# Graph attention weights as a larger of two products of exponentials, and the adjacency check on ScalarE

## The chip, the cores and the metric

The kernel runs on one core of one Trainium2 chip. The metric is the device time of a launch in microseconds, as the median of three runs. Lower is better. The core's engines are PE (TensorE: matrix products), DVE (VectorE), ACT (ScalarE), POOL (GpSimd) and SP (SyncE, which here only starts transfers); each works through its own list of instructions in order, and they meet through semaphores.

## The reference, cut to what matters

The input is x with 64 graphs of 256 nodes and 256 features, all fp32, and an adjacency of 0 and 1 (int32, about one in sixteen set). Two layers follow each other. Layer 0 runs two graph attentions, a norm, a feed-forward block and a norm. Layer 1 is an attention of eight heads in which the adjacency chooses among value matrices, again with a feed-forward block. The change concerns the graph attention and what the kernel must know of the adjacency:

```python
def _gat(h, adj, W, a, out_features):
    Wh = jnp.matmul(h, W)
    Wh1 = jnp.matmul(Wh, a[:out_features])
    Wh2 = jnp.matmul(Wh, a[out_features:])
    e = Wh1 + jnp.swapaxes(Wh2, 1, 2)
    e = jax.nn.leaky_relu(e, negative_slope=ALPHA)      # ALPHA = 0.2
    scores = jnp.where(adj > 0, e, NEG)
    att = jax.nn.softmax(scores, axis=1)
    return jnp.matmul(att, Wh)
```

So a weight is exp(max(t, 0.2 t)) with t = r + c, r a number of the row and c one of the column, times the adjacency, divided by its sum over the first node axis.

## The kernel before

The kernel has a quick path, `narrow_path`, which holds for adjacencies of 0 and 1 and for numbers that need no maximum subtracted, and a `general_path` for everything else. The quick path sums up on the way what tells whether it held: `other` collects the sums of a(a - 1) over the adjacency, `low`, `lowg` and `high` those of reciprocals and means. At the end the results of these sums decide whether the general path runs; with this input it doesn't.

The 64 graphs are taken in 32 pairs u. A pair is two graphs, so 512 nodes in T = 4 blocks of 128 partitions; NB = 2 blocks to a graph. Work is spread over three pairs at a time. The function `turn(y, x, z)` runs one turn: it does layer 1 of pair y, the feed-forward block of layer 0 of pair x = y + 1, and both graph attentions of pair z = y + 2. There are 32 turns; 30 have a pair z. An opening ahead of them brings the first two pairs so far.

Inside a turn the order of PE, SP, DVE and ACT is the order in which the code is written (`manual_schedule`), so each engine's list can be read off `turn`. In the opening only PE and SP follow the code; a scheduler orders DVE and ACT there.

A graph attention's softmax is the class `Softmax`. `score_rows` lays the row numbers r out in a bank of PSUM by four transposes (`rows`), a column number c per node stands in the projected features. `scores(b)` writes r + c for graph b (L741: ACT, Identity with the column as bias, one of 128x256 for each block) and takes the larger of it and 0.2 of it (L743: DVE, 128x512). `exp(b)` is L746 (ACT, 128x512). `masks(b)` multiplies by the transposed adjacency and sums along the way (L750: DVE, 128x256 for each block). `shares` takes the reciprocals (L754: DVE), and `scaled` multiplies the features by them (L766: ACT, four of 128x256).

In a turn with a pair z, this happens twice, each time in the middle of a feed-forward output. `HiddenOut` computes such an output with seven products instead of eight: `sums(n)` forms a sum of quarters on DVE (L946, 128x1024), `product(n)` is sixteen matmuls on PE (L960), `add(n)` adds a product to the output on DVE (L968); `out(n)` is a product and its add. Products share banks: 6 follows 1 in its bank, 7 follows 6, 4 follows 7, and 3 follows 5; each needs the add before it. Product 7 reads sum 3, product 3 reads sum 4.

First place (layer-1 attention of pair z, inside pair x's output): scores and exponentials stand at L1291 to 1294, then sum 4, products 2 and 5, the norm of y (`applied_norm`, L1300), masks, shares and scaling (L1302 to 1305), product 6, the features' transposes of y (`normed_features`: four transposes on DVE, L668, then copies on POOL and transfers from SP's and ACT's queues, L685 and L687), product 3, sum 3, and the products of the attention (`first_sums`, L775) with product 7 between their halves.

Second place (layer-2 attention, inside pair y's output): L1371 to 1396. Scores of both graphs lie among the adds of products 1 and 5, masks after product 2 and product 6, then shares and scaling. At the end come the check of the adjacency (`checked`, L706: one operation of 128x1024 on DVE), the loads of the next adjacency (eight transfers on SP, L449, into the tile that the check read and overwrote), and the products of the attention (`second_sums`, L786), whose result is normed for the next turn.

The other names that the prediction uses: L883 and L880 bring products of the first feed-forward half out of PSUM, L889 and L914 are its activation (gelu in layer 1, with a load of its table; exp needs another), L821 is the small operation `nm` of a norm, L986 are the query and key products (`qp`, `kp`) with which a turn begins, L988 their copies, L1021 the exponentials of the head attention.

Of the kernel before, what the change touches and what calls it, by code (L numbers as in the profile page):

```python
# [9 lines left out]
F32 = mybir.dt.float32  # L10
I32 = mybir.dt.int32
AF = mybir.ActivationFunctionType
ALU = mybir.AluOpType
# [3 lines left out]
P = 128  # L17
NEG = -9000000000000000.0
ALPHA = 0.2
# [366 lines left out]
def narrow_path(  # L386
# [13 lines left out]
    nc = tc.nc  # L400
    B, N, F = x.shape
# [5 lines left out]
    NB = N // P  # L407
    G = 2
    T = G * NB
    TN = G * N  # L410
    NG = B // G
# [7 lines left out]
    work = ctx.enter_context(tc.tile_pool(name="work", bufs=2))  # L419
# [50 lines left out]
    mhalf = const.tile([P, T], F32, name="mhalf")  # L470
# [10 lines left out]
    other = const.tile([P, NG], F32, name="other")  # L481
# [63 lines left out]
    g = {u: {} for u in range(NG)}  # L545
# [94 lines left out]
    def behind(*names):  # L640

        stack = ExitStack()
        for n in names:
            stack.enter_context(tc.issue_after(mark[n].ins))
        return stack
# [57 lines left out]

    def checked(u, aq):
        a = aq.rearrange("p t n -> p (t n)")
        nc.vector.scalar_tensor_tensor(a, a, 1.0, a, op0=ALU.subtract, op1=ALU.mult,  # L706
                                       accum_out=other[:, u:u + 1])

    def projected(u, hT, blocks, xp):
        if xp is None:  # L710
# [17 lines left out]
    class Softmax:  # L728

        def __init__(s, u, l, wh, rows, c):  # L730
            s.u, s.wh, s.rows, s.c = u, wh, rows, c
            s.s = (work.tile([P, T, N], F32, tag="s", name=f"s{u}_{l}", bufs=1) if u > 1 else
                   work.tile([P, 2 * T, N], F32, tag="e", name=f"s{u}_{l}")[:, :T])
            s.z = work.tile([P, T], F32, tag="z", name=f"z{u}_{l}")

        def block(s, b):
            return s.s[:, b * NB:(b + 1) * NB, :].rearrange("p t n -> p (t n)")

        def scores(s, b):
            for t in range(b * NB, (b + 1) * NB):  # L740
                nc.scalar.activation(s.s[:, t, :], s.rows[:, b * N:(b + 1) * N], AF.Identity,  # L741
                                     bias=s.wh[:, t, s.c:s.c + 1])
            nc.vector.scalar_tensor_tensor(s.block(b), s.block(b), ALPHA, s.block(b), op0=ALU.mult, op1=ALU.max)  # L743

        def exp(s, b):
            nc.scalar.activation(s.block(b), s.block(b), AF.Exp)  # L746

        def masks(s, b):
            for t in range(b * NB, (b + 1) * NB):
                nc.vector.scalar_tensor_tensor(s.s[:, t, :], s.s[:, t, :], 1.0, g[s.u]["aT"][:, t, :],  # L750
                                               op0=ALU.mult, op1=ALU.mult, accum_out=s.z[:, t:t + 1])
# [3 lines left out]
            nc.gpsimd.tensor_add(lowg, lowg, s.z)  # L755

        def all(s):
            for b in range(G):
                s.scores(b)
                s.exp(b)  # L760
                s.masks(b)
            s.shares()

# [27 lines left out]
    def normed(u, l, y, blocks=range(T)):  # L791

        applied_norm(y, *norm(u, l, y, blocks))

    def moments(u, l, y, blocks, mv=None):
        n = f"{u}_{l}_{blocks[0]}"
        st = work.tile([P, T, 6], F32, tag="st", name=f"st{n}", bufs=1)
        if mv is None:
            mv = work.tile([P, T, 2], F32, tag="mv", name=f"mv{n}")
        for t in blocks:  # L800
            nc.vector.bn_stats(st[:, t, :], y[:, t, :])  # L801
            nc.vector.bn_aggr(mv[:, t, :], st[:, t, :])  # L802
        return mv

    def norm(u, l, y, blocks=range(T), mv=None):

        n, t0 = f"{u}_{l}_{blocks[0]}", blocks[0]
        bt = slice(t0, t0 + len(blocks))
        mv = moments(u, l, y, blocks if mv is None else blocks[len(blocks) // 2:], mv)
        rs = work.tile([P, T], F32, tag="rs", name=f"rs{n}")  # L810
        nm = work.tile([P, T], F32, tag="nm", name=f"nm{n}")
        nc.gpsimd.tensor_scalar(rs[:, bt], mv[:, bt, 1], EPS, 0.0, op0=ALU.add, op1=ALU.add)  # L812
        nc.gpsimd.tensor_tensor(rs[:, bt], rs[:, bt], mhalf[:, bt], ALU.pow)  # L813
        if l == 3:
            nc.gpsimd.tensor_add(high[:, bt], high[:, bt], mv[:, bt, 0])
        return blocks, mv, rs, nm
# [279 lines left out]
    def first_sums(z, blocks=range(T)):  # L1096
        d = g[z]
        d["hp"] = gat_first(z, d["m"].s, d["xp"], None if blocks[0] == 0 else d["hp"], blocks)

    def second_sums(z, graphs=range(G)):  # L1100
        d = g[z]
        mv = None
        for b in graphs:
            add_blocks(z, "ygp", d["y"], b,
                       lambda t, k: d["m"].s[:, t // NB * NB + k, t % NB * P:(t % NB + 1) * P],
                       lambda b, k: d["hp"][:, b * NB + k, :F], NB)
            if b == 0 and len(graphs) == G:
                mv = moments(z, 0, d["y"], range(NB))
        return mv
# [45 lines left out]
    def turn(y_, x_, z):  # L1155
        Y, X, Z = (g.get(u) for u in (y_, x_, z))
# [41 lines left out]
        with order:  # L1198
# [70 lines left out]
            else:  # L1269
                n = norm(y_, 2, y, range(NB))  # L1270
# [13 lines left out]
            if Z:  # L1284
                n = norm(y_, 2, y, mv=mv)
            else:
                applied_norm(y, *n)
                n = norm(y_, 2, y, range(NB, T))
            if Z:
                out(1)  # L1290
                Z["m"].scores(0)  # L1291
                Z["m"].scores(1)
                Z["m"].exp(0)
                Z["m"].exp(1)
                out.sums(4)
                out(2, 5)
            elif X:
                out(5)
                out.sums(3)
# [30 lines left out]
            if X:  # L1330
                n = moments(x_, 1, X["y"], range(NB))
# [6 lines left out]
            if X:  # L1338
                out.add(4)
                n = norm(x_, 1, X["y"], mv=n)  # L1340
# [31 lines left out]
            out = HiddenOut(y_, 1, y, h1, w2s, out_sums(y_, 1))  # L1372
            out.product(1)
            out.sums(1, 2)
            Z["m"].scores(0)
            out.add(1)
            out.product(5)
            Z["m"].scores(1)
            Z["m"].exp(0)
            Z["m"].exp(1)  # L1380
            out.add(5)
            out.sums(4, 3)
            out(2)
# [5 lines left out]
            out(3)  # L1389
            affine(X["y"], rg2, rb2)  # L1390
            out(7)
            checked(z, Z["aq"])
            if z + 1 < NG:
                load_adjacency(z + 1)
            Z["n"] = norm(z, 0, Z["y"], mv=second_sums(z))
            out(4)
            waiting.append((y_, y))
# [3 lines left out]
    with tc.manual_schedule(engines={mybir.EngineType.PE, mybir.EngineType.SP}):  # L1401
        for stage in (early_first, project, first_softmax):
            stage(0)
        early_first(1)
        next(fold)
        for stage in (project, first_softmax):
            stage(1)
        first_sums(0)
        next(fold)
        second_softmax(0)  # L1410
        first_sums(1)
        next(fold)
        second_softmax(1)
        for b in range(G):
            second_sums(0, (b,))
            normed(0, 0, g[0]["y"], range(b * NB, (b + 1) * NB))
        next(fold)
        g[0]["hT"] = to_features(g[0]["y"], "h1T0")
        with behind("summed"):
            for u in range(2):  # L1420
                checked(u, g[u]["aq"])
        affine(g[0]["y"], rg1, rb1)
        load_x(2)
        load_rows(2)
        load_adjacency(2)
        first_hidden(0)("2a 1a 2b 1b 5a 5b 3a 3b 6a ra 6b rb 7a sa 7b sb 4a 4b")
        first = HiddenOut(0, 0, g[0]["y"], g[0]["h1"], wf2s, out_sums(0, 0))
        first.sums(1, 2, 4, 3)
        first(1, 2, 5, 6, 3)
        normed(0, 1, g[0]["y"], range(NB))  # L1430
        first(7, 4)
        normed(0, 1, g[0]["y"], range(NB, T))
        g[1]["n"] = norm(1, 0, g[1]["y"], mv=second_sums(1))
        g[0]["hT"] = to_features(g[0]["y"], "h2T0")
        affine(g[0]["y"], rg2, rb2)
        next(fold)
        for u in range(NG):
            turn(u, u + 1, u + 2)


    c = work.tile([P, 4], F32, tag="mv", name="checks")
    for n, v in enumerate((low, lowg, high, other)):
        nc.vector.tensor_reduce(c[:, n:n + 1], v, AX.X, ALU.add)
    s = work.tile([P, 1], F32, tag="ve", name="checked")
    nc.vector.tensor_reduce(s, c[:, 0:3], AX.X, ALU.add)
    good = work.tile([P, 2], F32, tag="z", name="good")
    nc.vector.tensor_scalar(good[:, 0:1], s, 1e30, None, op0=ALU.is_le)
    nc.vector.tensor_scalar(good[:, 1:2], c[:, 3:4], 0.0, None, op0=ALU.is_le)
    nc.vector.tensor_tensor(good[:, 0:1], good[:, 0:1], good[:, 1:2], ALU.mult)
    ps = bank("goodp")  # L1450
    nc.tensor.matmul(ps[:1, :1], good[:, 0:1], ones[:, 0:1], start=True, stop=True)
# [41 lines left out]
```

## Time and profile before

| what | value |
|---|---|
| median of 3 runs | 3076.99 us (3075.04 to 3077.49) |
| profiled execution, span | 3072.8 us, the only time that the page gives for it |
| median above the span | 4.2 us |
| PE busy | 3031.3 us, 99% |
| DVE busy | 2595.7 us, 84% |
| ACT busy | 1602.2 us, 52% |
| POOL busy | 648.0 us, 21% |
| a steady turn | 93.44 us (1331.4 to 1424.9) |
| L750, masks | 256 of 128x256, 97.1 us, mean 424 ns |
| L743, larger of two | 128 of 128x512, 92.4 us, mean 742 ns |
| L741, sums of row and column | 256 of 128x256, 100.2 us |
| L746, exponentials | 128 of 128x512, 76.5 us, mean 627 ns |
| L706, check of the adjacency | 32 of 128x1024, 38.9 us |

The profile is of one execution on the chip. Busy shares are averages over the span; the slices on its page cut the span into 40 parts and give the busy share of each in tenths. A line of the time line has start, duration, engine, line of the code, operation, output and input, shapes, count, and in brackets how long the engine stood idle before it and what ended that. Where operations follow each other without a wait, the next starts before the end of the one before, so in a row they cost less than their durations. PEld is the loading of the stationary operand, which runs ahead of the matmuls.

### The profile page before, as it was taken

What the parts mean: (1) busy time and instruction counts of PE and PEld (TensorE: products, weight loads), DVE (VectorE), ACT (ScalarE), POOL (GpSimd) and SP (SyncE); (2) the same over time, 40 slices, a digit from 0 to 9 for tenths busy, and PEclk for the clock granted to TensorE, in tenths of its full rate; (3) what the DMA queues carried; (4) which work ended last, traced back from release to release, by engine and by line L of the source; (5) the groups of instructions that cost most, each with busy time, mean ns of one, the idle gap of its engine ahead of it and who ended that gap; (6) DMA issues with size and microseconds to landing.
All of it is one profiled execution on the core that took longest, in us unless ns stands there. A gap on an engine that the chain in (4) does not pass through costs nothing.

```text
span 3072.8 us, 56424 instructions
## 1 busy us (share of the span) xinstructions
PE 3031.3 (99%) x21432; PEld 2330.1 (76%) x21432; DVE 2595.7 (84%) x4890; ACT 1602.2 (52%) x3212; POOL 648.0 (21%) x896
## 2 busy tenths in 40 slices
PE   7999999999999999999999999999999999999998
PEld 6677877778777778777787777787777787777866
DVE  4788888888888888888888888888888888888876
ACT  4455545555545555555555455555455554554553
POOL 3122121222211221212221112222112212122211
PEclk8999999999999999999999999999999999999999
DMA  5011111211111211112211112111112111121000
GB/s 149 13 37 35 34 39 25 44 41 35 35 35 32 44 37 32 39 26 43 44 33 35 40 25 44 37 36 35 30 38 44 35 34 39 25 44 37 18 13 16
DMA packets 427988, 113.37 MB, mean 37 GB/s; under 512 B 364568, under 2 KB 427072, under 8 KB 427712
## 3 DMA queue, kind: packets, MB, share of 16 engines
q1 hardware_dynamic: 417664, 102.46, 15.8%
q10 hardware_dynamic: 8992, 6.19, 0.8%
q8 instruction: 172, 2.82, 0.4%
q0 software_dynamic: 1056, 1.05, 0.1%
q14 instruction: 104, 0.85, 0.1%
HBM read 57.04 MB, written 16.78 MB: 24 GB/s over the span
## 4 chain that ended last, share of the span: by engine, by line
PE 90%; DVE 7%; DMA 1%; POOL 1%; ACT 1%; issue 0%; SPq 0%; ACTq 0%; POOLq 0%; DVEq 0%
PE yf L960 22%; PE h1a L871 15%; PE h1b L871 11%; PE po L1041 8%; PE vp L999 7%; PE sp L1015 4%; PE xpp L715 4%; PE yop L786 4%; PE qp L986 3%; PE kp L986 3%; PE ygp L786 3%; PE zo L1044 2%; PE hpp L775 2%; DVE s L750 2%; DVE yt L668 1%; DVE eaq L946 1%
## 5 line engine op out<-in xcount | busy, mean ns | idle before, releaser
L880 ACT COPY h<-h1b 128x512 f32<-128x512 f32 x384 | 224.6, 585 | 390.0 <-PE h1b L871 390.0
L828 ACT ACTIVATE y<-y,nm,rs 128x256 f32<-128x256 f32 x450 | 239.0, 591 | 238.4 <-DVE nm L821 234.1
L883 DVE TENSOR_TENSOR h<-h1a,h 128x512 f32<-128x512 f32 x384 | 263.6, 687 | 117.5 <-PE h1a L871 111.6
L1026 DVE TENSOR_TENSOR ea<-e,aT 128x1024 f32<-128x1024 f32 x256 | 309.5, 1239 | 54.3 <-ACT e L1021 54.3
L1021 ACT ACTIVATE e<-sp 128x512 f32<-128x512 f32 x512 | 264.3, 602 | 52.0 <-PE sp L1015 48.7
L1054 POOL TENSOR_TENSOR low<-low,rq 128x16 f32<-128x16 f32 x64 | 13.9, 218 | 1087.3 <-DVE rq L1053 1087.3
L685 POOL COPY hT<-yt 32x256 f32<-32x256 f32 x244 | 207.2, 849 | 59.0 <-DVE yt L668 51.4
L968 DVE TENSOR_TENSOR y<-yf,y 128x256 f32<-128x256 f32 x448 | 183.1, 409 | 39.7 <-PE yf L960 39.6
L999 PE MATMUL vp<-wv,hT 128*128 128x512 f32 x480 | 214.0, 599 | 0.0
L801 DVE BATCH_NORM_STATS2 st<-y 128x6 f32<-128x256 f32 x512 | 207.7, 408 | 5.5
L812 POOL TENSOR_SCALAR rs<-mv 128x4 f32<-128x4 f32 (+1 forms) x134 | 34.2, 255 | 720.7 <-DVE mv L802 454.6
L999 PEld LDWEIGHTS vp<-wv,hT 128*128 128x128 f32 x480 | 88.7, 190 | 110.4 <-issue 103.2
L840 DVE TENSOR_TENSOR y<-y,rb 128x1024 f32<-128x1024 f32 (+1 forms) x130 | 166.9, 1284 | 3.2
L988 ACT ACTIVATE q<-qp,cols 128x512 f32<-128x512 f32 x64 | 44.0, 687 | 238.3 <-PE qp L986 238.3
L914 ACT ACTIVATE h<-h,cols 128x512 f32<-128x512 f32 x256 | 167.0, 714 | 1.5 <-DVE h L883 1.1
L837 DVE TENSOR_TENSOR y<-y,rg 128x1024 f32<-128x1024 f32 (+1 forms) x130 | 161.8, 1245 | 2.2 <-ACT y L828 1.1
L1031 DVE TENSOR_TENSOR es<-e 128x1024 f32<-128x1024 f32 x128 | 155.5, 1215 | 0.0
L677 POOL COPY hT<-yt 32x256 f32<-32x256 f32 x120 | 115.6, 964 | 169.2 <-DVE yt L668 159.7
L1015 PEld LDWEIGHTS sp<-q,k 32*128 32x128 f32 x2048 | 92.5, 184 | 74.2 <-issue 44.8
L1015 PE MATMUL sp<-q,k 32*128 32x256 f32 x2048 | 146.6, 400 | 2.0 <-ACT k L988 2.0
L1041 PE MATMUL po<-e,v 128*32 128x256 f32 x2048 | 136.3, 384 | 0.0
L813 POOL TENSOR_TENSOR rs<-rs,mhalf 128x4 f32<-128x4 f32 (+1 forms) x134 | 134.5, 1004 | 8.2
(249 smaller groups left out, 7191.4 us busy)
## 6 DMA issues: line engine op xcount, KB each, us to landing
hT<-yt SPq DMA_DIRECT2D x912, 32.0 KB, 2.0
y<-in_x_dram SPq DMA_DIRECT2D x32, 512.0 KB, 4.7
xq<-in_x_dram SPq DMA_DIRECT2D x240, 64.0 KB, 2.2
aq<-in_adj_dram SPq DMA_DIRECT2D x240, 64.0 KB, 2.4
out_dram<-y SPq DMA_DIRECT2D x30, 512.0 KB, 2.9
hT<-yt ACTq DMA_DIRECT2D x180, 32.0 KB, 1.9
wf<-in_L_gnn_w_ff_dram SPq DMA_DIRECT2D x2, 1024.0 KB, 8.1
w<-in_L_gnn_W_dram SPq DMA_DIRECT2D x2, 1024.0 KB
```

Of the source, the lines that this page charges most:

```text
L786: nc.tensor.matmul(ps[:, i * F:(i + 1) * F], lhs(t, k), rhs(b, k), start=(k == 0), stop=(k == n - 1))
L801: nc.vector.bn_stats(st[:, t, :], y[:, t, :])
L828: mark["normed"] = nc.scalar.activation(y[:, t, :], y[:, t, :], AF.Identity, bias=nm[:, t:t + 1], scale=rs[:, t:t + 1])
L871: nc.tensor.matmul(ps[:, i * N:(i + 1) * N], w_[:, f * P:(f + 1) * P], m, start=first and i == 0, stop=True, skip_group_check=True)
L880: mark["copied"] = nc.scalar.copy(out(h, o, b), pair(ps))
L883: mark["added"] = nc.vector.tensor_tensor(out(h, o, b), pair(one[h]), out(h, o, b), ALU.add)
L960: nc.tensor.matmul(s.ps[n][:, i * F2:(i + 1) * F2], a[:, k, i * P:(i + 1) * P], w_[:, k, :], start=n in (1, 2, 5) and i == 0 and k == 0, s ...
L999: nc.tensor.matmul(ps, hT[k][:, t * P:(t + 1) * P], wvf[:, k, :], start=(k == 0), stop=(k == KB - 1))
L1015: nc.tensor.matmul(ps[a][:, j * N:(j + 1) * N], k_[hp, m, j0:j0 + P], q[hp, m, b * N:(b + 1) * N], start=True, stop=True)
L1021: mark[f"exp{b * KB + m}"] = nc.scalar.activation(e[:, a, :], ps[a], AF.Exp, scale=isd)
L1026: nc.vector.tensor_tensor(ea[:, a:a + 2, :], e[:, a:a + 2, :], ab[:, None, :].to_broadcast([P, 2, NB * N]), ALU.mult)
L1041: nc.tensor.matmul(po[hp, m * N:(m + 1) * N], vs[:, hp], w[:, a, j * N:(j + 1) * N], start=(n == 0), stop=(n == len(terms) - 1))
```

## The change

The weight is written with exponentials apart. With E = exp(r) and E' = exp(0.2 r) of the rows and f = exp((0.2 - 1) c) of the columns,

exp(max(t, 0.2 t)) = max(exp(r) exp(c), exp(0.2 r) exp(0.2 c)) = exp(c) max(E, E' f),

and exp(c), the same for all that is summed over, drops out in the softmax. So ACT takes one exponential of 4 columns (f) and two of 128x512 (E and E', both graphs at once), and DVE takes max(E' f, E) for each block of 128x256 in one operation. The sums on ACT, the exponentials of full blocks and the maxima of 128x512 go. The four products stand in `masks`, ahead of the masks of the same graph. The new tile `es` shares the two buffers of the head attention's node sums.

The check becomes a Square on ACT: (a - 0.5) squared is 0.25 for 0 and 1 and more for any other integer, so the sum is compared with a quarter of the number of elements. In a turn it moves ahead, behind the exponentials of the second place, and with it the loads of the next adjacency on SP; in the opening it no longer waits to be placed behind a sum.

```diff
     def checked(u, aq):
         a = aq.rearrange("p t n -> p (t n)")
-        nc.vector.scalar_tensor_tensor(a, a, 1.0, a, op0=ALU.subtract, op1=ALU.mult,
-                                       accum_out=other[:, u:u + 1])
+        nc.scalar.activation(a, a, AF.Square, bias=mhalf[:, 0:1], accum_out=other[:, u:u + 1])
...
+            s.e = work.tile([P, 2, TN], F32, tag="es", name=f"er{u}_{l}")
+            s.f = work.tile([P, T], F32, tag="ef", name=f"ef{u}_{l}")
+
+        def exps(s):
+            nc.scalar.activation(s.f, s.wh[:, :, s.c], AF.Exp, scale=ALPHA - 1.0)
+            nc.scalar.activation(s.e[:, 0], s.rows, AF.Exp)
+            nc.scalar.activation(s.e[:, 1], s.rows, AF.Exp, scale=ALPHA)
...
-        def scores(s, b):
+        def masks(s, b):
+            bn = slice(b * N, (b + 1) * N)
             for t in range(b * NB, (b + 1) * NB):
-                nc.scalar.activation(s.s[:, t, :], s.rows[:, b * N:(b + 1) * N], AF.Identity,
-                                     bias=s.wh[:, t, s.c:s.c + 1])
-            nc.vector.scalar_tensor_tensor(s.block(b), s.block(b), ALPHA, s.block(b), op0=ALU.mult, op1=ALU.max)
-
-        def exp(s, b):
-            nc.scalar.activation(s.block(b), s.block(b), AF.Exp)
-
-        def masks(s, b):
+                nc.vector.scalar_tensor_tensor(s.s[:, t, :], s.e[:, 1, bn], s.f[:, t:t + 1], s.e[:, 0, bn],
+                                               op0=ALU.mult, op1=ALU.max)
             for t in range(b * NB, (b + 1) * NB):
                 nc.vector.scalar_tensor_tensor(s.s[:, t, :], s.s[:, t, :], 1.0, g[s.u]["aT"][:, t, :],
                                                op0=ALU.mult, op1=ALU.mult, accum_out=s.z[:, t:t + 1])
...
                 out(1)
-                Z["m"].scores(0)
-                Z["m"].scores(1)
-                Z["m"].exp(0)
-                Z["m"].exp(1)
+                Z["m"].exps()
                 out.sums(4)
                 out(2, 5)
...
             out.sums(1, 2)
-            Z["m"].scores(0)
+            Z["m"].exps()
+            checked(z, Z["aq"])
+            if z + 1 < NG:
+                load_adjacency(z + 1)
             out.add(1)
             out.product(5)
-            Z["m"].scores(1)
-            Z["m"].exp(0)
-            Z["m"].exp(1)
             out.add(5)
...
             out(7)
-            checked(z, Z["aq"])
-            if z + 1 < NG:
-                load_adjacency(z + 1)
             Z["n"] = norm(z, 0, Z["y"], mv=second_sums(z))
...
-        with behind("summed"):
-            for u in range(2):
-                checked(u, g[u]["aq"])
+        for u in range(2):
+            checked(u, g[u]["aq"])
...
-    nc.vector.tensor_scalar(good[:, 1:2], c[:, 3:4], 0.0, None, op0=ALU.is_le)
+    nc.vector.tensor_scalar(good[:, 1:2], c[:, 3:4], 0.25 * NG * T * N, None, op0=ALU.is_le)
```

More of the change, by code (lines that the diff above doesn't have):

```diff
@@ L734, in __init__ @@
             s.z = work.tile([P, T], F32, tag="z", name=f"z{u}_{l}")
-        def block(s, b):
-            return s.s[:, b * NB:(b + 1) * NB, :].rearrange("p t n -> p (t n)")
-        def scores(s, b):
-            for t in range(b * NB, (b + 1) * NB):
-                nc.scalar.activation(s.s[:, t, :], s.rows[:, b * N:(b + 1) * N], AF.Identity,
-                                     bias=s.wh[:, t, s.c:s.c + 1])
-            nc.vector.scalar_tensor_tensor(s.block(b), s.block(b), ALPHA, s.block(b), op0=ALU.mult, op1=ALU.max)
-        def exp(s, b):
-            nc.scalar.activation(s.block(b), s.block(b), AF.Exp)
-        def masks(s, b):
+            s.e = work.tile([P, 2, TN], F32, tag="es", name=f"er{u}_{l}")
[6 more added lines that the diff above has]
+            bn = slice(b * N, (b + 1) * N)
+            for t in range(b * NB, (b + 1) * NB):
+                nc.vector.scalar_tensor_tensor(s.s[:, t, :], s.e[:, 1, bn], s.f[:, t:t + 1], s.e[:, 0, bn],
+                                               op0=ALU.mult, op1=ALU.max)
             for t in range(b * NB, (b + 1) * NB):
@@ L757, in all @@
         def all(s):
+            s.exps()
             for b in range(G):
-                s.scores(b)
-                s.exp(b)
                 s.masks(b)
```

## The prediction

> **What bounds the kernel now.** I read the page first (busy shares and slices), then the waits by engine, then the time line of one steady turn, 1331 to 1425 us, engine by engine.
>
> ```profile
> span 3072.8 us, 56424 instructions
> PE 3031.3 (99%) x21432; PEld 2330.1 (76%) x21432; DVE 2595.7 (84%) x4890; ACT 1602.2 (52%) x3212; POOL 648.0 (21%) x896
> PE   7999999999999999999999999999999999999998
> PEclk8999999999999999999999999999999999999999
> ```
>
> PE is the bound from slice 2 on, at full clock. It has 41.5 us of idle time in all and most of that lies in the opening. A turn takes 93.44 us, so a stall of PE in a turn is not won back later: PE has no slack to win it from. The question is therefore only where PE waits, and for whom, in the two places where a turn runs a graph softmax. The waits give one that repeats in every turn of that kind:
>
> ```profile
> PEld yf L960 <- DVE eaq L946: 15.0, 30, 0.5
> ```
>
> Thirty times, once per turn with a third pair Z. The windows show that it reaches PE itself (columns after the width: PE, PEld, DVE, ACT, POOL busy, then clock, DMA share, GB/s):
>
> ```profile
> 1380.30:1382.29 1.99, 1.90 (x10) 1.33 (x8) 1.99 (x5) 0.83 (x3) 1.48 (x2) 1.00 0.13 30
> 1400.32:1411.51 11.19, 11.19 (x101) 11.19 (x100) 10.62 (x22) 7.30 (x16) 4.07 (x5) 1.00 0.25 38
> ```
>
> DVE is busy for all of the first stretch and PE for 1.90 of 1.99 us; in the second PE never waits. The time line of the first place, the layer-1 softmax:
>
> ```profile
> 1376.92 0.42 DVE L968 TENSOR_TENSOR y<-yf,y 128x256 f32<-128x256 f32 x1 [0.48 <-PE yf L960]
> 1377.33 0.42 DVE L750 SCALAR_TENSOR_TENSOR s<-s,aT 128x256 f32<-128x256 f32 x1
> 1378.83 0.18 DVE L754 RECIPROCAL z<-z 128x4 f32<-128x4 f32 x1
> 1379.43 1.70 ACT L766 ACTIVATE xp<-xp,z 128x258 f32<-128x258 f32 x4
> 1380.30 1.91 PE L775 MATMUL hpp<-xp,s 128*128 128x258 f32 x8
> 1380.88 1.36 DVE L946 TENSOR_TENSOR eaq<-h 128x1024 f32<-128x1024 f32 x1
> 1382.29 1.86 PEld L960 LDWEIGHTS yf<-wf,eaq 128*128 128x128 f32 x16 [0.50 <-DVE eaq L946]
> ```
>
> From the add at 1376.92 on DVE runs without a gap until the quarter sum ends at 1382.24, and product 7 starts at 1382.29. The twin group of eight hpp matmuls goes 1384.18 to 1385.92, 1.74 us; here it is 1.99 to the next start, so PE loses 0.25 us. Anything put on DVE between 1377 and 1382 moves product 7 one for one.
>
> The second place, the layer-2 softmax:
>
> ```profile
> 1404.36 1.95 PE L960 MATMUL yf<-w,h 128*128 128x128 f32 x16
> 1410.10 0.18 DVE L754 RECIPROCAL z<-z 128x4 f32<-128x4 f32 x1
> 1410.31 1.71 ACT L766 ACTIVATE hp<-hp,z 128x256 f32<-128x256 f32 x4 [3.86 <-DVE z L754]
> 1411.51 3.62 PE L786 MATMUL ygp<-hp,s 128*128 128x256 f32 x16
> 1413.23 1.22 DVE L706 SCALAR_TENSOR_TENSOR aq<-aq 128x1024 int32<-128x1024 int32 x1
> ```
>
> The first scaled block of hp is there at 1410.31 + 0.49 = 1410.80, PE wants it at 1411.51: 0.71 us of cover, some 0.66 after a hop of 0.05 (the gap from quarter sum to product 7).
>
> **What the Trainium skill says.** "VectorE: DVE Perf Modes", section "The perf-mode tier table": an operation with two fp32 tensors in SBUF runs at one element a cycle. The trace agrees for this operation, median by line:
>
> ```profile
> L743 DVE SCALAR_TENSOR_TENSOR s<-s x128: 674/682/1642, 24.9 to 2900.9; 128x512 f32<-128x512 f32 x128
> L750 DVE SCALAR_TENSOR_TENSOR s<-s,aT x256: 404/416/1487, 26.7 to 2905.8; 128x256 f32<-128x256 f32 x128
> ```
>
> (682 - 416) / 256 = 1.04 ns an element. Splitting 512 into two of 256 thus costs the fixed part once more: in a row, 0.345 us per 256 (1377.33, 1377.68, 1378.02) against 0.60 per 512. "SBUF — State Buffer", section "SBUF: two separate sides": a DVE operation with two SBUF inputs and a GpSimd one that reads SBUF exclude each other. The maxima 1642 and 1487 lie in the opening beside POOL's weight sums; in the two places POOL is idle while the masks run. "TensorE: Matmul & The Clock Gate", section "What's actually happening": the clock is halved after an idle window of about 3.4 us; the stalls below are shorter, and after a wait of 1.43 us at 95.88 this trace still shows clock 1.00. "ScalarE: Activation LUTs", section "What ACT_TABLE_LOAD costs", prices the new activations below; its 1283 ns for a table load is what L914 and L746 show, and its 613 ns for 512 columns stands beside 602 on L1021.
>
> **The change part by part.** PE's order in the turns is unchanged; DVE, ACT and SP follow the written order.
>
> 1. ACT, scores and exponentials. Gone per softmax: four Identity (4 x 0.39) and two Exp (about 1.2). New: Exp over 4 columns (estimate from the page: 186 + 0.833 x 4 = 0.19 us) and two Exp of 128x512 (0.60 each, as the rows of L1021). Place 1: rows are there at 1371.5, exps done by 1372.9, wanted at 1377.33. Place 2: gelu ends 1402.54, the table load (1.28) now comes first, exps done about 1405.2, wanted at 1407.5. Cost on the path: nothing, hidden by 4.5 and 2.3 us of ACT's own idle time. Loads stay two per turn. The score rows' bank is held about 1 us longer; its next user comes six banks later.
>
> 2. DVE, the leaky maxima go, eight 128x256 operations stand where four stood. Place 1: gone at 1373.69, 1.20 us; but the add at 1376.92 waits for PE's product 5, so this only makes its wait longer (0.48 to about 1.7). The four new products lie behind that add, in front of the masks: 4 x 0.345 = 1.38 us. The reciprocal moves from 1378.83 to 1380.21, ACT's scaling from 1379.43 to 1380.42, its first block is done at 1380.91, hpp starts at 1380.95 in place of 1380.30. Behind the reciprocal DVE has the add, four transposes, an add and the quarter sum, 3.41 us as now: 1383.62, product 7 at 1383.67. **PE: +1.38 us a turn**, in two stalls of 0.65 and 0.7 to 1. The features' DMAs, ACT's and SP's issues of them, behind the scaling and the transposes, move by the same 1.4 us, as does PE, so no new wait there. 30 x 1.38 = 41.4 us.
>
> 3. Place 2: before, from 1403.62 DVE had leaky 0.80, add, leaky 0.60, add, two sums. Now the second add waits for product 5, done when the next product starts, 1404.36 + 0.20 (the offset of the add at 1376.92). Add to 1404.89, sums 2.27, add 0.34: masks from 1407.50. Four operations 1.37, add 0.34, four 1.37, 0.11: reciprocal at 1410.69, 0.59 later than 1410.10. The cover is 0.66. Cost 0 to 0.1 us a turn, I take 0.05: 1.5 us. Product 7 there needs the add at 1408.9 + 0.41, before 1409.73: as now.
>
> 4. The check: DVE loses 1.15 us at 1413.23, ACT gains a Square of 128x1024 (estimate from that page: 280 + 0.833 x 1024 = 1.13 us) at 1405.2, ahead of the scaling at 1410.9: hidden by 4.5 us. Nothing is won: what follows on DVE ends in nm, done at 1419.76, and ACT uses it only at 1420.97, behind the second copy of qp. That is 1.2 us of cover; without it the gain would be 1.15 a turn. The adjacency loads, eight behind it on SP, start at about 1409 rather than 1414.5, behind the feature DMAs already issued; the next on that queue is due at 1423.7. Nothing.
>
> 5. The opening, four softmaxes on the latency path: fewer hops between ACT and DVE, but all maxima now behind the last Exp, four more DVE operations each, partly locked by POOL (1.5 us each there), and the second pair's feature copy queued behind eight of them. Bounds -2 to +4 us, I take +1. The check there leaves DVE at 62 to 65.6, where nm waits for POOL anyway.
>
> Sum on the span: 41.4 + 1.5 + 1 = 44 us: 3072.8 becomes 3117. The median of the runs lies 4.2 above the span: 3121, taken as 3122. Unknown: a multiply whose scalar is a column, which no DVE row shows. On ACT a column bias costs 0.09 (475 ns for L741, 386 for L717). Between 0 and 0.09 I take nearly 0. At 0.09: 0.36 a turn in place 1 and 0.3 to 0.36 in place 2, 20 us, 3142.
>
> **Rivals.** (a) Both places stall: the column scalar or a pause between product and mask uses up the 0.07 us left in place 2. For it: the thin cover. Against: mask follows its own product by two operations. 3128 to 3150, 20%. (b) Part of place 1 is hidden, the new products cheaper or the wait at product 7 not DVE's alone: 3084 to 3115, 8%. (c) Hidden, PE has room I don't see: 3071 to 3083, 6%. (d) Faster, on the other side: the check's 1.15 us on DVE is what PE really follows at the end of the turn, 30 x 1.15 = 34.5 us, 3042. It decides only if nm were later than ACT's second qp copy (it is 1.2 us earlier) and if eight operations ended by 1379.0 as four do now. 3%. That the change does not do what it says I rule out: the new orders show it.
>
> **How the numbers follow.** The main case, 3115 to 3128, has 63%. Main and most of (a) with the top of (b) make the range 3113 to 3143. A change under 0.2%, 6 us, can't be told from none here. Slower: 63 + 20 + 8 = 91%; same 6%; faster 3%.
>
> **What would show it.** Right: turns of 94.8 to 95 us; PE waiting for ACT's scaled xp ahead of hpp (about 0.65) and for the quarter sum ahead of product 7 (about 1); DVE's wait at the add of product 5 near 1.7; eight operations of 0.41. Wrong: turns of 93.4 with no wait at hpp; products above 0.45 us; a PE wait ahead of ygp over 0.2 us, which is (a).

## The result and the profile after

The changed kernel takes 3130.48 us (median of four runs, 3130.06 to 3133.3), the kernel before, run beside it, 3077.24 us (3075.04 to 3077.71). The recorded ratio is 1.0179, with a 95% interval of 1.0165 to 1.0193 (the two medians alone give 1.0173): slower by 53 us. The profiled execution spans 3128.4 us, 55.6 more than before. Its page, busy shares and two rows of the slices:

```profile
span 3128.4 us, 56357 instructions
PE 3045.5 (97%) x21432; PEld 2330.0 (74%) x21432; DVE 2593.8 (83%) x4954; ACT 1549.8 (50%) x3084; POOL 637.1 (20%) x896
PE   7999999999999999999999999999999999999998
PEclk8999999999999999999999999999999999999999
```

PE issues the same 21432 matmuls, and its clock row is the same as before. Its idle time has gone from 41.5 to 82.9 us and its busy time up by 14, which together is the growth of the span. DVE is busy for as long as before, although 64 more operations run on it, and ACT for 52 us less, which has won nothing. The waits of the kernel after name the places:

```profile
PE hpp L772 <- ACT xp L763: 22.0, 30, 0.7
PE yf L957 <- DVE eaq L943: 20.4, 30, 0.7
PEld ygp L783 <- ACT hp L763: 6.4, 30, 0.2
```

Each stands there thirty times, once per turn with a pair Z. The first two lie in the first place, where before only the weight load waited (15.0 us in all); the third is in the second place. The time line of the first place, with the columns as before:

```profile
1398.79 0.42 DVE L965 TENSOR_TENSOR y<-yf,y 128x256 f32<-128x256 f32 x1 [0.23 <-PE yf L957]
1400.58 0.42 DVE L965 TENSOR_TENSOR y<-yf,y 128x256 f32<-128x256 f32 x1 [1.36 <-PE yf L957]
1400.99 0.88 DVE L745 SCALAR_TENSOR_TENSOR s<-er,ef 128x256 f32<-128x256 f32 x2
1401.78 0.42 DVE L748 SCALAR_TENSOR_TENSOR s<-s,aT 128x256 f32<-128x256 f32 x1
1404.07 0.18 DVE L752 RECIPROCAL z<-z 128x4 f32<-128x4 f32 x1
1404.28 1.72 ACT L763 ACTIVATE xp<-xp,z 128x258 f32<-128x258 f32 x4 [1.09 <-DVE z L752]
1404.84 2.01 PE L772 MATMUL hpp<-xp,s 128*128 128x258 f32 x8 [0.73 <-ACT xp L763]
1406.12 1.36 DVE L943 TENSOR_TENSOR eaq<-h 128x1024 f32<-128x1024 f32 x1
1407.53 2.05 PE L957 MATMUL yf<-wf,eaq 128*128 128x128 f32 x16 [0.68 <-DVE eaq L943]
```

The chain reads from top to bottom. DVE stands idle for 1.36 us ahead of product 5's add, since that add waits for PE. Only behind it do the new products (L745) begin; two of them take 0.79 us up to the first mask (L748), so 0.395 each. From the start of this add to the reciprocal pass 3.49 us (1400.58 to 1404.07); before, it was 1.91 (1376.92 to 1378.83). hpp starts late, then product 7. Measured from the transposes of the score rows (1394.58 here, 1370.92 before), hpp starts at 10.26 in place of 9.38 and product 7 at 12.95 in place of 11.37: 1.58 us of a turn.

The time line of the second place:

```profile
1429.80 0.42 DVE L965 TENSOR_TENSOR y<-yf,y 128x256 f32<-128x256 f32 x1 [0.54 <-PE yf L957]
1436.16 0.18 DVE L752 RECIPROCAL z<-z 128x4 f32<-128x4 f32 x1
1436.37 1.71 ACT L763 ACTIVATE hp<-hp,z 128x256 f32<-128x256 f32 x4 [4.97 <-DVE z L752]
1436.93 3.32 PEld L783 LDWEIGHTS ygp<-hp,s 128*128 128x128 f32 x16 [0.21 <-ACT hp L763]
```

Here the score rows begin at 1425.56 (before 1400.32). The reciprocal is at 10.60 in place of 9.78, so 0.82 later, and ygp at 11.37 in place of 11.19. So the start of ygp moves by 0.18 only, but by the next product the loss is 0.28, and some 0.06 comes behind it. By line, the new operation beside the masks (shortest, median and longest duration in ns):

```profile
L745 DVE SCALAR_TENSOR_TENSOR s<-er,ef x256: 472/479/1482, 24.8 to 2960.9; 128x256 f32<-128x256 f32 x128
L748 DVE SCALAR_TENSOR_TENSOR s<-s,aT x256: 409/421/1486, 25.6 to 2961.7; 128x256 f32<-128x256 f32 x128
```

A turn takes 95.37 us in place of 93.44 (median distance of the score rows from one turn to the next): 1.58 + 0.28 + 0.06 = 1.92, against 1.93. Thirty turns give 58 us; the span grew by 55.6, and the first value products start 1.6 us earlier than before (114.56, before 116.16).

### The profile page after: what moved, and what is told of

Same layout as the page of the kernel before. It is cut to its first block, busy times and chain, and to the rows that moved or that the text cites. A ratio compares the mean times of both kernels' runs of the same rounds, so it can differ in the third digit from the quotient of the medians.

```text
span 3128.4 us, 56357 instructions
## 1 busy us (share of the span) xinstructions
PE 3045.5 (97%) x21432; PEld 2330.0 (74%) x21432; DVE 2593.8 (83%) x4954; ACT 1549.8 (50%) x3084; POOL 637.1 (20%) x896
## 4 chain that ended last, share of the span: by engine, by line
PE 89%; DVE 8%; ACT 1%; DMA 1%; POOL 1%; issue 0%; SPq 0%; ACTq 0%; POOLq 0%; DVEq 0%
PE yf L957 22%; PE h1a L868 15%; PE h1b L868 11%; PE po L1038 7%; PE vp L996 7%; PE sp L1012 4%; PE xpp L714 4%; PE ygp L783 4%; PE yop L783 4%; PE qp L983 3%; PE kp L983 3%; PE zo L1041 2%; DVE s L745 2%; PE hpp L772 2%; DVE s L748 2%; DVE eaq L943 1%
## 5 line engine op out<-in xcount | busy, mean ns | idle before, releaser
L685 POOL COPY hT<-yt 32x256 f32<-32x256 f32 x244 | 207.8, 852 | 76.4 <-PE hpp L772 44.4
L668 DVE STREAM_TRANSPOSE yt<-y 128x256 f32<-128x256 f32 x364 | 139.5, 422 | 14.8 <-ACT y L825 10.6
L957 PE MATMUL yf<-wf,eaq 128*128 128x128 f32 x1024 | 127.6, 278 | 21.5 <-DVE eaq L943 20.4
L772 PE MATMUL hpp<-xp,s 128*128 128x258 f32 x512 | 126.4, 391 | 22.0 <-ACT xp L763 22.0
```

Of the source, the lines that this page charges most:

```text
L957: nc.tensor.matmul(s.ps[n][:, i * F2:(i + 1) * F2], a[:, k, i * P:(i + 1) * P], w_[:, k, :], start=n in (1, 2, 5) and i == 0 and k == 0, s ...
```

## The experiments

All times are medians, with the kernel before run on the same chip between them (3074.4 to 3074.7 us in the four groups of runs). The turn is the median distance of the score rows' transposes from turn to turn in the profiled execution, which is steadier than the time.

| kernel | us | ratio to before, 95% interval | turn, us |
|---|---|---|---|
| first place alone | 3120.86 | 1.0150 [1.0133, 1.0167] | 95.02 |
| second place alone | 3084.76 | 1.0033 [1.0021, 1.0044] | 93.78 |
| check alone | 3072.13 | 0.9993 [0.9984, 1.0002] | 93.44 |
| both softmaxes, old check | 3133.81 | 1.0194 [1.0177, 1.0211] | 95.36 |
| constant for the column | 3115.20 | 1.0130 [1.0114, 1.0145] | 94.87 |
| early products | 3086.78 | 1.0039 [1.0024, 1.0055] | 93.90 |
| and by graph | 3079.78 | 1.0016 [1.0010, 1.0023] | 93.63 |
| and first place filled | 3073.67 | 0.9996 [0.9988, 1.0005] | 93.32 |
| old softmax, masks early | 3071.08 | 0.9989 [0.9982, 0.9995] | 93.25 |
| filled, old opening | 3070.34 | 0.9989 [0.9980, 0.9997] | 93.33 |
| and transposes early | 3074.43 | 1.0001 [0.9993, 1.0010] | 93.37 |

### The parts alone

Three kernels do one part of the change each, a fourth does all but the check. In the first two the old class stays for the opening and the other place:

```diff
 # first place alone (Apart is the new class)
-        d["m"] = Softmax(z, 0, d["xp"], ...)
+        d["m"] = (Apart if z > 1 else Softmax)(z, 0, d["xp"], ...)
...
-                Z["m"].scores(0)
-                Z["m"].scores(1)
-                Z["m"].exp(0)
-                Z["m"].exp(1)
+                Z["m"].exps()
                 out.sums(4)
```

> The kernel before with the new softmax in the first place of the turns alone (layer 1, inside pair x's output); second place, check and opening as before. My theory (the four products stand behind product 5's add and move product 7 one for one): 4 x 0.395 = 1.58 us a turn, 30 turns, +47 us, so 3122 to 3127; a wait of PE at hpp on ACT's scaling near 0.7. Rival, that the new place of the exponentials or the missing POOL and ACT work matters and the products only share in it: +20 to +35, 3097 to 3112. Rival, that part of it was hidden and the second place or the check made the loss: under +10.

It takes 46.3 us more than before (3120.86 against 3074.56), as the theory's +47; the numbers of the expectation were counted from 3077. The waits of PE in this kernel:

```profile
PE hpp L813 <- ACT xp L804: 22.0, 30, 0.7
PE yf L998 <- DVE eaq L984: 20.5, 30, 0.7
```

These are the two waits of the changed kernel, nearly to the tenth. The turn is 1.58 longer, all of it up to product 7. The first place alone makes the larger part of the loss.

```diff
 # second place alone
-        d["m"] = Softmax(z, 1, d["hp"], ...)
+        d["m"] = (Apart if z > 1 else Softmax)(z, 1, d["hp"], ...)
...
-            Z["m"].scores(0)
+            Z["m"].exps()
             out.add(1)
             out.product(5)
-            Z["m"].scores(1)
-            Z["m"].exp(0)
-            Z["m"].exp(1)
             out.add(5)
```

> The kernel before with the new softmax in the second place of the turns alone (layer 2); first place, check and opening as before. My theory (reciprocal 0.82 us later against a cover of 0.66, with a little more behind it): 0.2 to 0.35 us a turn, +6 to +10 us, 3083 to 3088, with a wait ahead of ygp on ACT's scaled hp of about 0.2. Rival, that this place is covered and what the turn lost beyond the first place comes from the check's new place: 3075 to 3079. Rival, that the second place alone stalls by all that the reciprocal moved: +25, 3101.

+10.2 us, just above the theory's +6 to +10; the turn is 0.34 longer. The wait ahead of ygp is there:

```profile
PEld ygp L824 <- ACT hp L804: 6.2, 30, 0.2
```

The rival with 25 us falls: of the 0.82 by which the reciprocal is later, the cover takes most.

```diff
 # check alone
     def checked(u, aq):
-        nc.vector.scalar_tensor_tensor(a, a, 1.0, a, op0=ALU.subtract, op1=ALU.mult, accum_out=other[:, u:u + 1])
+        nc.scalar.activation(a, a, AF.Square, bias=mhalf[:, 0:1], accum_out=other[:, u:u + 1])
...
             Z["m"].exp(0)
             Z["m"].exp(1)
+            checked(z, Z["aq"])
+            if z + 1 < NG:
+                load_adjacency(z + 1)
             out.add(5)
...
             out(7)
-            checked(z, Z["aq"])
-            if z + 1 < NG:
-                load_adjacency(z + 1)
...
-        with behind("summed"):
-            for u in range(2):
-                checked(u, g[u]["aq"])
+        for u in range(2):
+            checked(u, g[u]["aq"])
...
-    nc.vector.tensor_scalar(good[:, 1:2], c[:, 3:4], 0.0, None, op0=ALU.is_le)
+    nc.vector.tensor_scalar(good[:, 1:2], c[:, 3:4], 0.25 * NG * T * N, None, op0=ALU.is_le)
```

> The kernel before with the adjacency check as a Square on ScalarE, at its new place in the turn and with the adjacency loads behind it, and in the opening without the delay; both softmaxes as before. My theory: DVE's 1.2 us at that place were covered, so nothing is won in the turns, and the opening may move by a microsecond or two: 3075 to 3079. Rival (d) of the prediction, that the check's time on DVE is what PE follows: 3042. Rival, that the Square or the earlier loads delay something on ACT or SP: 3082 or more.

-2.4 us, a little outside what was expected, with an interval that takes in no change. The turn is exactly as long as before, 93.44, so if the 2 us are real, they lie in the opening. Rival (d), which wanted 3042, is out: taking 1.2 us of every turn off DVE wins nothing there.

```diff
 # both softmaxes, old check: the changed kernel with (opening and limit of the sum put back too)
-        nc.scalar.activation(a, a, AF.Square, bias=mhalf[:, 0:1], accum_out=other[:, u:u + 1])
+        nc.vector.scalar_tensor_tensor(a, a, 1.0, a, op0=ALU.subtract, op1=ALU.mult, accum_out=other[:, u:u + 1])
...
             Z["m"].exps()
-            checked(z, Z["aq"])
-            if z + 1 < NG:
-                load_adjacency(z + 1)
...
             out(7)
+            checked(z, Z["aq"])
+            if z + 1 < NG:
+                load_adjacency(z + 1)
```

> The changed kernel with the adjacency check back on VectorE in its old place, loads and opening's delay too; both softmaxes new. My theory (the loss is the softmaxes' alone): 3128 to 3133, as the changed kernel. If the check on ACT or its loads cost something: 3122 or less. If the check's removal from DVE won something that the softmaxes hid: 3138 or more. With the other three runs it shows whether the parts add up.

3133.81, 0.8 above the range of the theory; the turn is that of the changed kernel (95.36). The parts add up: by turns 1.58 + 0.34 + 0.00 = 1.92 against 1.93, by times 46.3 + 10.2 - 2.4 = 54.1 against 53.

### The price of the column scalar

```diff
-                nc.vector.scalar_tensor_tensor(s.s[:, t, :], s.e[:, 1, bn], s.f[:, t:t + 1], s.e[:, 0, bn],
+                nc.vector.scalar_tensor_tensor(s.s[:, t, :], s.e[:, 1, bn], 0.8, s.e[:, 0, bn],
                                                op0=ALU.mult, op1=ALU.max)
```

> The changed kernel with the constant 0.8 in place of the column f[:, t] in all products; it leaves out the column factor of the attention weights, nothing else, so its output is another one. My theory, that the column scalar has a price of its own, 0.05 us an operation beside the masks' pitch of 0.345: four operations in the first place give back 0.2, the second place 0.2 to 0.25 a turn, together 12 to 14 us: 3116 to 3121. Rival, that the products are longer because of what they read (two different tiles) and not because of the column: no change, 3128 to 3133.

3115.2, 15.3 us under the changed kernel and 0.8 below the range of the theory. The same operation in this kernel, by line, and two of them with the mask behind them on the time line:

```profile
L745 DVE SCALAR_TENSOR_TENSOR s<-er x256: 408/416/1482, 24.7 to 2950.4; 128x256 f32<-128x256 f32 x128
1398.95 0.76 DVE L745 SCALAR_TENSOR_TENSOR s<-er 128x256 f32<-128x256 f32 x2
1399.62 0.42 DVE L748 SCALAR_TENSOR_TENSOR s<-s,aT 128x256 f32<-128x256 f32 x1
```

416 ns in place of 479, with the same two tensors read: the 63 ns are the column's, not the tiles'. In a row two products now take 0.67 us up to the first mask (1398.95 to 1399.62), so 0.335 each in place of 0.395. The column's price in a row is thus 0.06 us, not the 0.05 of the expectation, which had taken the masks' pitch of 0.345 for that of a product without a column. The turn falls by 0.50, from 95.37 to 94.87, eight times that price. Product 7 is then 1.34 late, and hardly 0.1 is lost in the second place, whose wait ahead of ygp is gone. The longest, 1482 ns, stays without the column, so it is not the column's. It lies in the opening: it starts at 45.45, while an operation of POOL on weights runs from 45.21 to 46.66, and ends at 46.93. That agrees with the Trainium skill ("SBUF — State Buffer", section "SBUF: two separate sides"): a DVE operation with two SBUF inputs and a GpSimd one that reads SBUF keep each other out.

### The order of DVE's list

If the loss comes from where the products stand, it must go when they move, with not an operation fewer. The first place has 1.36 us of idle DVE ahead of product 5's add, and the exponentials are ready by then.

```diff
                 Z["m"].exps()
                 out.sums(4)
-                out(2, 5)
+                out(2)
+                Z["m"].products(0)
+                Z["m"].products(1)
+                out(5)
...
-                Z["m"].masks(0)
-                Z["m"].masks(1)
+                Z["m"].masks(0, False)      # without its products
+                Z["m"].masks(1, False)
```

> The changed kernel with the four products of the first place ahead of product 5's add, where DVE waits for PE for 1.36 us, in place of behind it; the same operations, masks where they were. My theory, that the loss lies in the order of DVE's queue and not in the amount of its work: the wait takes 1.36 of the 1.58 us, so about 0.2 to 0.3 a turn remain of the first place's loss, 3084 to 3092. Rival, that eight operations of DVE in this stretch cost the same wherever they stand, because DVE is full there: over 3120.

3086.78: 44 of the 53 us are back, and the turn is down from 95.37 to 93.90, thirty times 1.47. The time line of this kernel (DVE, then PE):

```profile
1380.28 0.42 DVE L969 TENSOR_TENSOR y<-yf,y 128x256 f32<-128x256 f32 x1 [0.23 <-PE yf L961]
1380.62 1.66 DVE L745 SCALAR_TENSOR_TENSOR s<-er,ef 128x256 f32<-128x256 f32 x4
1382.20 0.41 DVE L969 TENSOR_TENSOR y<-yf,y 128x256 f32<-128x256 f32 x1
1385.44 1.91 PE L776 MATMUL hpp<-xp,s 128*128 128x258 f32 x8
1387.57 2.05 PE L961 MATMUL yf<-wf,eaq 128*128 128x128 f32 x16 [0.22 <-DVE eaq L947]
```

Here `products(b)` is the part of `masks(b)` that forms the larger of the two products. The four fill the place of the wait; the add behind them no longer waits, and comes 0.13 late. hpp starts at 9.37 from the score rows (1376.07), as before the change; product 7 at 11.50, the 0.13 late. DVE was not full in this stretch, it stood in the wrong order.

For the second place, reciprocal and scaling are done for each graph apart:

```diff
             Z["m"].masks(0)
+            Z["m"].shares(0)
+            Z["m"].scaled(F, 0)
             out(6)
             Z["m"].masks(1)
-            Z["m"].shares()
-            Z["m"].scaled(F)
+            Z["m"].shares(1)
+            Z["m"].scaled(F, 1)
```

> As the run with the early products, and in the second place reciprocal and scaling done for each graph apart, so that hp's first blocks wait for their own graph's masks only. My theory, that ygp waits for the one reciprocal over both graphs: the 0.3 us a turn of the second place go, 8 to 10 us less than with the early products alone, 3075 to 3083. Rival, that the second place's loss lies in DVE's adds behind the masks: as the early products alone, or a little slower for the two more small operations.

7.0 us less than with the early products alone (3079.78), 1 under the expected 8 to 10. The turn falls by 0.27, to 93.63, and no wait ahead of ygp is left. What remains over before, 0.19, is the 0.13 at product 7 and 0.06 in the rest of the turn.

Then the first place is filled altogether:

```diff
-                out(1)
+                out.product(1)
                 Z["m"].exps()
                 out.sums(4)
-                out(2)
+                out.add(1)
                 Z["m"].products(0)
+                out(2)
                 Z["m"].products(1)
+                Z["m"].masks(0, False)
                 out(5)
...
-                Z["m"].masks(0, False)
                 Z["m"].masks(1, False)
```

> As the run by graph, with the first place filled: sum 4 ahead of add 1, the first graph's products ahead of product 2's add, the second graph's products and the first graph's masks ahead of product 5's add. My theory: behind add 5 then stand only two masks where the kernel before had four, so the stall of about 0.25 us a turn that the kernel before had at product 7 goes as well: 3064 to 3071, faster than the kernel before by 0.1 to 0.3 percent. Rival, that the adds moved back make PE wait for banks: 3075 or more.

3073.67: no slower than before, but not the 3064 to 3071 that was expected. Product 7 now starts at 11.18, 0.19 earlier than before the change, and the median turn is 93.32, 0.12 less than before. Yet the mean turn is 93.45, and that of the kernel before 93.49. In three of the 30 turns the next stage's first products (h1b) start 0.4 to 1.3 us later than in the others, in two by 0.1. One such turn on the time line, on DVE and on PE:

```profile
1760.07 0.42 DVE L856 TENSOR_TENSOR tt<-hT 128x256 f32<-128x256 f32 x1 [2.60 <-DMA hT<-yt]
1760.20 1.10 PE L873 MATMUL h1b<-hT,w 128*128 128x256 f32 x4 [1.17 <-issue]
```

DVE waits 2.60 us for the transfers of the transposed features hT, and h1b, which reads the same features, starts 0.13 after DVE does. In the kernel before, h1b is never more than 0.34 later than in most turns. Its stall at product 7 gives the transfers 0.19 more time, which explains a part of the difference; the rest is that the features come later in these turns of the filled kernel than in the same turns of the kernel before.

### Does it need the new softmax, and what holds the last stage?

The same gap can be used with the old softmax, on top of the check on ScalarE; and the filled turn can be had with the old opening.

```diff
 # old softmax, masks early: check alone, with
                 out.sums(4)
-                out(2, 5)
+                out(2)
+                Z["m"].masks(0)
+                out(5)
...
-                Z["m"].masks(0)
                 Z["m"].masks(1)
```

> The kernel before with the check on ScalarE, and in the first place the first graph's two masks ahead of product 5's add; the old softmax everywhere. If the stall of some 0.2 us that the kernel before has at product 7 were worth its length, 30 turns would give 5 us on top of what the check alone showed: 3066 to 3068. My theory, from the run with the first place filled: the next wait is for the transposed features, so that the turn takes 93.4 us again and only the check's part shows: 3070 to 3073.

3071.08, in the range of the theory. The median turn is 93.25, but four turns start h1b 0.4 to 1.5 us late, and the mean is 93.43 again. One of them:

```profile
1385.26 0.43 DVE L853 TENSOR_TENSOR tt<-hT 128x256 f32<-128x256 f32 x1 [2.09 <-DMA hT<-yt]
1385.40 1.10 PE L870 MATMUL h1b<-hT,w 128*128 128x256 f32 x4 [0.67 <-PE yf L959]
```

So this limit comes with either softmax. PE's wait is put down to its own product, but that had ended; DVE's line shows the features landing.

```diff
 # filled, old opening: first place filled, with
-        d["m"] = Softmax(z, 0, d["xp"], ...)
+        d["m"] = (Apart if z > 1 else Softmax)(z, 0, d["xp"], ...)
...
-        d["m"] = Softmax(z, 1, d["hp"], ...)
+        d["m"] = (Apart if z > 1 else Softmax)(z, 1, d["hp"], ...)
```

> The turns of the run with the first place filled (new softmax, its own order, check on ScalarE), and the old softmax for the first two pairs in the opening. My theory: the turns take 93.4 us as before, the opening gives the 2 us that the check alone gave there: 3070 to 3073. Rival, that the opening's new softmaxes cost nothing: as the run with the first place filled, 3073 to 3075.

3070.34 us, faster than before by 0.1%, with an interval of 0.9980 to 0.9997. It and the one above are the only two of the eleven kernels whose interval lies below one, and by the prediction's own measure a change under 0.2% can't be told from none. Its turns are those of the filled kernel (mean 93.44); whether the 3 us between the two come from the opening isn't settled, since the two spans differ by only 0.4 (3070.8 and 3071.2).

Last, a try at the late features: their transposes go ahead of product 6's add, which waits for PE.

```diff
-                out(6)
+                out.product(6)
                 if Z:
                     hT = normed_features(y_, 2, y, queues=(nc.sync, nc.scalar))
+                out.add(6)
```

> The kernel of the run with the first place filled and the old opening, and in the first place the four transposes of pair y's features ahead of product 6's add, which waits for PE. My theory, that in the filled turn the first products of the next stage wait for these features, so that the 0.2 us that product 7 no longer loses is given back there: the features come 0.5 to 0.7 us earlier, the turn takes 93.2 to 93.3, and the time is 3 to 5 us less than without the change: 3065 to 3068. Rival, that something else sets the start of that stage (PE's own matmuls, a bank, the next sum's place on DVE): 3069 to 3073.

3074.43: the theory fell, and the time lies above the rival's range too. The transposes start 0.75 us earlier in the turn (7.38 from the score rows, against 8.13 in the filled kernel), but only the first of the features' transfers follow. In the median turn the first transfer is issued at 9.18, without the edit at 9.57; the last one at 13.16, without it at 13.19; and DVE begins to read the features no earlier, at 15.47 against 15.43. They still come late in single turns. The waits of PE have it:

```profile
PE h1b L913 <- DMA hT<-yt: 2.3, 2, 1.3
```

So starting the transposes earlier doesn't help here, and it hardly moves the last transfers. What makes transfers late in single turns isn't shown, but the traces give a hint. In the filled kernel and the three after it, 20 of 120 turns start h1b more than 0.05 us late. In 19 of these 20 a packet of 16 KB, of the queue whose kind the profile gives as "instruction", starts between 10.0 and 13.5 us from the score rows, just while the features are issued and moved; only 28 of the 120 turns have such a packet there. For the late turn of the filled kernel shown above, the DMA view of 1752.3 to 1755.8 has it (packets, MB, share of 16 engines), while the turn before has none in that stretch:

```profile
q8 instruction: 1, 0.02, 2.1%
```

This packet took 1.18 us. No run moves these packets: that they go together with the late features is seen, that they are the cause isn't shown.

## Why the prediction was right, and by how much it wasn't

The sign and the size came out: 3130 in a range of 3113 to 3143. But the likeliest case (3115 to 3128) missed it by 2.5 us, and what came was rival (a), both places stalling, by its own first reason, the column scalar. By the steps:

1. **ACT costs nothing: right.** The exponentials over four columns take 0.21 us (0.19 estimated) and the rows' 0.60. The wait at hpp is for the scaling, which waits for DVE, and nothing waits in the turns for the new exponentials.
2. **First place: mechanism right, term mis-sized.** The add's wait grew from 0.48 to 1.36 (1.7 was said; most of the rest shows as a new wait of 0.23 at the add before it). The two stalls, 0.73 and 0.68, stand where they were put. But a turn loses 1.58, not 1.38: four products follow each other at 0.395 us, not 0.345. With a constant in the column's place it is 1.34, four times 0.335: the pitch of 0.345, read from the masks, was a little high for a product without a column.
3. **Second place: the term failed.** The reciprocal was put 0.59 later against 0.66 of cover, so 0.05 was taken. It is 0.82 later; with a constant it is 0.56 later, so the columns add 0.26, about four times 0.06. The loss is 0.28 at the product behind ygp and 0.34 by the end of the turn. Only 0.18 of it is the later start of ygp, which is all that the prediction counted; what makes the rest is open. With a constant the whole turn loses 1.43, of which 1.34 is the first place's: 0.09, near the 0.05 of the prediction.
4. **The check and the loads: right.** Nothing won and nothing lost in the turn. The Square took 1.149 us (1.13 estimated), with 0.199 for a second instruction that reads the sum out; the estimate lacked that, and ACT's idle time hid it.
5. **The opening: within its bounds.** -2 to +4 was given and +1 taken; the first value products came 1.6 us earlier. Single executions of one kernel differ by more than that (the filled one took 3070.49 to 3077.80), so this part is known to some microseconds only.

The term that decided is thus one: "Between 0 and 0.09 I take nearly 0." Measured, the column costs 0.06 in a row of products, 0.50 us a turn over eight of them, 15 us in thirty turns. Without it a turn loses 1.43 us, and the prediction's own sum for that case was 1.38 + 0.05 = 1.43. That the two agree to the hundredth is luck, since the first place comes out 0.04 lower and the second 0.04 higher than said. Such a kernel takes 3115.2 us, not the 3121 of the prediction. Its addition of 4.2 us for the median above the span was wrong too: it set the median beside the span of another execution. In every execution for which the record has both, the time is 1.6 to 1.8 us above its own span. This addition and the opening, both put too high, made up for some 5 of the 15 us, which is luck too.

Rivals (b) and (c), a hidden part, fell with the first place alone, which gave 46 us. Rival (d) fell with the check alone.

## What to carry to other kernels

Where an engine's order is fixed, the place of an operation decides what it costs. The same four products cost 1.58 us a turn behind an add that waits for TensorE, and 0.13 ahead of it, where VectorE would have stood idle. So ask of every new operation when its inputs are ready, and put it into the last idle stretch before a wait, not where its predecessor happened to stand. And where a stall of a few tenths is taken out of a pipeline that runs at 99%, look for what is late next: here the median turn fell by 0.12 us and the mean by less than 0.05, since single late transfers gave the rest back.

## What the runs showed of the hardware that was not expected

- A VectorE operation of 128x256 fp32 with two SBUF tensors takes 479 ns with a column as its scalar and 416 ns with a constant. In a row the pitch is 0.395 against 0.335 us.
- A sum taken along with an activation is a second instruction on ScalarE, 0.199 us behind a Square of 128x1024 that takes 1.149 us.
- Twelve transfers of 32 KB that bring transposed features are on time in most turns, and in three or four of 30 late enough to hold TensorE for 0.4 to 1.5 us once the turn leaves them no time. The 18th and the 25th turn are among them in three of the four kernels with such a turn, so it isn't chance alone. A 16 KB packet of an instruction queue lies beside the transfers in 19 of the 20 turns that are late by more than 0.05; that it is the cause isn't shown.
